# A mixer's decay matrix: from products on TensorE to rows loaded on all partitions and a bias per head

## The chip, the cores and the metric

The kernel runs on one core of a Trainium2 chip. The metric is the device time of one execution in microseconds (us). A core has five engines that run their own instruction streams in order: PE (TensorE, with its weight loads shown apart as PEld), DVE (VectorE), ACT (ScalarE), POOL (GpSimd) and SP (SyncE, which here issues nearly all DMAs). PE writes its results to PSUM, eight banks of 2 KB per partition; the other data lie in SBUF, 128 partitions wide, or in DRAM.

## The reference

The model has two layers on x of 16 sequences x 128 tokens x 256 channels, with a context of the same shape. Layer 0 is an mLSTM mixer with the context as keys and values, then a mixture of experts (two shared experts and the best two of eight). Layer 1 is a cross attention of 16 heads, then a mixture of sixteen experts. The change concerns the first mixer. For each of 16 batches and 8 heads of 32 channels it computes, with q the normed x and k = v = the context:

```
cs        = cumsum(log_sigmoid(fg))                  # per head, along the 128 tokens
log_D     = cs[s] - cs[t] + ig[t], only t <= s       # else -inf
D         = exp(log_D - max_t log_D)                 # the decay matrix, 128 x 128
C         = (q k' / sqrt(32)) * D
h         = C / (max(|sum C|, exp(-max log_D)) + 1e-6) @ v
x         = x + tanh(g) * layernorm(h) * ln_scale
```

With a[t] = ig[t] - cs[t] the row maximum is cs[s] + m[s], where m is the running maximum of a. So D[t, s] = exp(a[t] - m[s]) for t <= s, and the factor 1/sqrt(32) goes into the exponent as -0.5 log 32.

## The kernel before

The 16 batches lie in four groups g of four. The first stage is one loop over steps b from -4 to 22. Step b works on batch b's scores (`mlstm_scores`, `mlstm_products`), batch b-1's values (`mlstm_values`, `mlstm_back`) and batch b-2's end (`mlstm_close`). Between these, at three places of each step (`run(b, 0)`, `run(b, 1)`, `run(b, 2)`), stand units that `at(step, place, ...)` has entered: the layer norms of a group (`ln_stats`, `apply1`, `ln_turn`), its gates (`gate_proj`, `gate_act`, `gate_scan`, `gate_spread`), the keys and values of layer 1 (`k_proj`, `v_proj`), the shared experts' pieces (`shared_gate`, `shared_up`, `shared_down`) and, from step 18, the routing of layer 0 (`route0`, moved on by `pump0`). The order is written by hand: within `manual_schedule` each of PE, DVE, ACT and POOL executes its instructions in the order in which the program writes them. SP has its DMAs in program order too.

The decay matrix is made with products. `gate_scan` builds, for a group, a tile `la` with the rows a and 1 (eight rows for each batch, in strips of 32 partitions), and a tile that `gate_spread` spreads by DVE over the heads (`rb`, L409). For a batch, two products over a strip's rows give a[t] - m[s] for four heads each in one PSUM bank (`lp0`, `lp1`, L459). A product in bf16 of the identity with the mask `caus` adds -1e30 where t > s (L462). ACT takes the exponential of a bank into SBUF (`dm`, L467). Then `mlstm_products` (L481, L487) makes q k' of half the heads in banks `qp0` and `qp1`, and DVE multiplies by `dm` into `ct`.

```
nc.tensor.matmul(t, la[rows, :], rb[rows, ...], start=True, stop=False)   # L459
nc.tensor.matmul(t, identb, caus, start=False, stop=True)                 # L462
nc.scalar.activation(t, lp[j], AF.Exp)                                    # L467
nc.vector.tensor_tensor(half[0], qp[j], half[1], ALU.mult)                # L487
```

PSUM has two banks tagged `tp` (transposes, gates, values), two tagged `e` (k, v and shared pieces), `lp0`, `lp1`, `qp0`, `qp1`. An fp32 product is two MATMUL instructions in the trace.

After the loop come the 39 expert tiles of layer 0 (`tile_in`, `tile_up`, `tile_down`; L851 in `lp` and `qp` banks, L869 in `e`), the last shared pieces, and layer 1. The expert weights' DMAs (L815) are issued at step 17, where the mixer's tiles are given up. Loads of the first stage are all issued at the start: x, the context by group (`load_c`) and by batch (`load_v`, then two steps ahead), the shared experts' weights (3 MB) and small ones.

Of the kernel before, what the change touches and what calls it, by code (L numbers as in the profile page):

```python
# [12 lines left out]
F32 = mybir.dt.float32  # L13
# [54 lines left out]
def flamingo_kernel(ctx: ExitStack, tc: tile.TileContext, a: dict, out: bass.AP):  # L68
# [9 lines left out]
    identb = cst.tile([P, P], BF16, name="identb")  # L78
    make_identity(nc, identb)
# [3 lines left out]
    caus = cst.tile([P, 4, P], BF16, name="caus")  # L83
# [3 lines left out]
        pattern=[[0, 4], [1, P]], channel_multiplier=-1,  # L87
# [67 lines left out]
    def new_xnT(g):  # L155
        return res.tile([P, KC, TG], F32, tag="xnT", name="xnT", bufs=3)
# [80 lines left out]
    load_c(2)  # L237
# [6 lines left out]
    for e in range(NSH):  # L244
# [8 lines left out]
    for g in range(2, G):  # L253
        load_x(g)
# [6 lines left out]

    xn_d = dr.tile([B * S, D], F32, name="xn_d")
# [19 lines left out]

    e32 = s1c.tile([P, 32], F32, name="e32")
    nc.vector.tensor_reduce(e32, ident.rearrange("p (i c) -> p c i", c=32), AX.X, ALU.add)
    rowm = s1c.tile([P, 3], F32, name="rowm")
    nc.vector.tensor_reduce(rowm[:, 0:1], e32[:, 0:NH0], AX.X, ALU.add)
    nc.vector.tensor_reduce(rowm[:, 1:2], e32[:, NH0 : 2 * NH0], AX.X, ALU.add)
    first, second, add_a = (rowm[:, i : i + 1] for i in range(3))  # L290

    nc.vector.scalar_tensor_tensor(add_a, second, -0.5 * math.log(DH0), first, ALU.mult, ALU.add)

    hsel = s1c.tile([P, 2, NH0 // 2], F32, name="hsel")
    nc.vector.tensor_tensor(
        hsel, e32[:, NH0 : 2 * NH0].rearrange("p (k j) -> p j k", j=2),
        e32[:, 0:NH0].rearrange("p (k j) -> p j k", j=2), ALU.subtract,
    )
# [92 lines left out]
    def gate_scan(g):  # L391
# [7 lines left out]
        la = s1.tile([P, S], F32, name="la")  # L399
        nc.vector.tensor_scalar(la, av, second, add_a, ALU.mult, ALU.add)  # L400
        nc.vector.tensor_tensor(cs, cs, mx, ALU.add)
        nc.vector.tensor_scalar(mx, mx, first, second, ALU.mult, ALU.add)
        gate_g[g] = (la, mx, cs)

    def gate_spread(g):
        la, mx, m = gate_g[g]
        rb = s1.tile([P, NH0, S], F32, name="rb")
        hs = hsel.rearrange("p j k -> p (j k)")
        nc.vector.tensor_tensor(  # L409
            rb, mx.unsqueeze(1).to_broadcast([P, NH0, S]), bc(hs, [P, NH0, S]), ALU.mult  # L410
        )
        mt = s2p.tile([P, P], F32, tag="tp", name="mt", bufs=2)
        nc.tensor.transpose(mt, m, ident)
        en = s1.tile([P, GB, 32], F32, name="en")
        nc.scalar.activation(en.rearrange("p i r -> p (i r)"), mt, AF.Exp, scale=-1.0)
        gate_g[g] = (la, rb, en)

    def k_proj(g, o):
        ps = s2p.tile([P, TG], F32, tag="e", name="kps", bufs=2)
# [12 lines left out]
    def v_proj(g, pr):  # L432
        ps = s2p.tile([P, 2, D], F32, tag="e", name="vps", bufs=2)
# [18 lines left out]
    def mlstm_scores(b):  # L452
        g, i = divmod(b, GB)
        la, rb, _ = gate_g[g]
        rows = ts(i, 32)
        lp = []
        for j in range(2):
            t = s2p.tile([P, NH0 // 2, S], F32, tag=f"lp{j}", name="lp")
            nc.tensor.matmul(  # L459
                t, la[rows, :], rb[rows, j * NH0 // 2 : (j + 1) * NH0 // 2, :], start=True, stop=False  # L460
            )
            nc.tensor.matmul(t, identb, caus, start=False, stop=True)  # L462
            lp.append(t)
        dm = []
        for j in range(2):
            t = s1.tile([P, NH0 // 2, S], F32, tag="dm", name="dm", bufs=2)
            nc.scalar.activation(t, lp[j], AF.Exp)  # L467
            dm.append(t)
        ct = [s1.tile([P, NH0 // 2, S], F32, tag="ct", name="ct", bufs=4) for j in range(2)]
        hT_b[b] = (dm, ct)  # L470
        mlstm_products(b, 0)

    def mlstm_products(b, ph):

        g, i = divmod(b, GB)
        dm, ct = hT_b[b]
        qp = [s2p.tile([P, NH0 // 2, S], F32, tag=f"qp{j}", name="qp")[:, 0:KC, :] for j in range(2)]
        for c in range(KC):
            for j in range(2):
                rows = ts(2 * ph + j, DH0)  # L480
                nc.tensor.matmul(  # L481
                    qp[j][:, c, :], cx_g[g][rows, c, ts(i, S)], xnT_g[1, g][rows, c, ts(i, S)],
                    start=True, stop=True,
                )
        for j in range(2):
            half = [t.rearrange("p (c h) s -> p h c s", h=2)[:, ph] for t in (ct[j], dm[j])]
            nc.vector.tensor_tensor(half[0], qp[j], half[1], ALU.mult)  # L487
        if ph == 1:
            hT_b[b] = ct

    def mlstm_values(b):
# [3 lines left out]
        for k in range(NH0 // 2):  # L495
            for j in range(2):
                nc.tensor.matmul(  # L497
                    hp[ts(j, 2 * DH0), k, :], vv[:, 2 * k + j, :], ct[j][:, k, :],
# [6 lines left out]
    def mlstm_back(b):  # L505
# [5 lines left out]
        en = gate_g[g][2][:, i, 0:NH0]  # L511
# [27 lines left out]
    def shared_gate(g, f):  # L539
        e, f_ = divmod(f, HC0)  # L540
        gp = s2p.tile([P, TG], F32, tag="e", name="gp", bufs=2)
# [8 lines left out]
    def shared_up(g, f):  # L550
        e, f_ = divmod(f, HC0)
        up = s2p.tile([P, TG], F32, tag="e", name="up", bufs=2)
# [8 lines left out]
    def shared_down(g, e, t):  # L561
        yp = s2p.tile([P, D], F32, tag="e", name="yp", bufs=2)
# [30 lines left out]
    def route0():  # L593
# [11 lines left out]
        pre = s2p.tile([P, B, E0], F32, tag="lp0", name="pre")  # L605
# [990 lines left out]
```

## Time and profile before

| | us |
|---|---|
| median of three runs | 1031.11 (1023.12 to 1031.48) |
| the profiled execution's own time | 1025.47 |
| its span in the trace | 1023.8 |
| PE busy | 937.5 (92%) |
| PE weight loads | 564.5 (55%) |
| DVE busy | 481.6 (47%) |
| ACT busy | 347.0 (34%) |
| POOL busy | 216.7 (21%) |
| mean granted TensorE clock | 0.939 of full speed |

Busy time is the time in which at least one instruction of the engine ran. A group's row gives busy time in us and mean ns of one instruction, then the engine's idle time just before them and what ended it. The granted clock is the share of full speed that PE had. A window's row gives a stretch, its length, and for each engine busy time and number of instructions in it.

The first lp product starts at 28.1 us and the last batch's at 262.5 us; the first expert tile's products start at 347 us, the first gather of layer 0's results is at 588.5 us.

### The profile page before, as it was taken

To read this page: it belongs to the slowest core of one execution; us is meant where nothing else is said; L and a number is where in the kernel's file an instruction comes from. 1 tells how busy PE (TensorE), PEld (TensorE's weight loads), DVE (VectorE), ACT (ScalarE), POOL (GpSimd) and SP (SyncE) were. 2 spreads that over 40 slices of the span, in tenths; PEclk is the share of its full clock that TensorE was granted. 3 is DMA by queue.
4 is the path that set the end of the run, shared out by engine and by line. 5 is a ranking of instruction groups with operands and counts; after the bars stand their busy time and mean duration, and the time that the engine had idled before them with its cause. 6 is when DMAs were issued, how large, how long until landed. Compare 5 with 4: busy or idle time off the path is not lost.

```text
span 1023.8 us, 13944 instructions
## 1 busy us (share of the span) xinstructions
PE 937.5 (92%) x4510; PEld 564.5 (55%) x4524; DVE 481.6 (47%) x1756; ACT 347.0 (34%) x807; POOL 216.7 (21%) x318
## 2 busy tenths in 40 slices
PE   4999999999998999999999987979889898988996
PEld 2555555655554556656655554545555555555553
DVE  2555454434336422222222145786858665733534
ACT  2342424233210221121122115665454433544540
POOL 3122011001000211111110043432110233053505
PEclk9896999898999999999999995989989799999998
DMA  8692100000049211111111048113000002243523
GB/s 274 233 309 87 61 6 31 6 6 21 1 160 353 86 52 44 47 46 42 47 47 32 26 132 299 43 31 105 21 21 1 23 33 81 77 135 117 175 71 118
DMA packets 63510, 89.59 MB, mean 88 GB/s; under 512 B 9328, under 2 KB 48880, under 8 KB 62928
## 3 DMA queue, kind: packets, MB, share of 16 engines
q1 hardware_dynamic: 56960, 70.74, 20.9%
q0 software_dynamic: 6480, 17.97, 5.7%
q8 instruction: 38, 0.62, 0.3%
q14 instruction: 32, 0.26, 0.1%
HBM read 56.26 MB, written 32.42 MB: 87 GB/s over the span
## 4 chain that ended last, share of the span: by engine, by line
PE 78%; DVE 10%; issue 4%; ACT 4%; DMA 2%; POOL 1%; SPq 1%; POOLq 0%; DVEq 0%; ACTq 0%
PE typ L869 7%; PE tgp L851 7%; PE tup L851 7%; PE gp L543 6%; PE gu L1317 6%; PE yp L564 5%; PE up L554 5%; PE lp L459 3%; PE tp L1039 3%; PE yp L1346 3%; PE sp L1013 3%; PE qp L481 2%; PE yps L1107 2%; PE hp L497 2%; PE ln_tp L355 2%
## 5 line engine op out<-in xcount | busy, mean ns | idle before, releaser
L1032 ACT ACTIVATE sc<-sc,mx 128x128 f32<-128x128 f32 x256 | 78.3, 388 | 41.2 <-DVE mx L1026 41.2
L822 POOL DMA_INDIRECT xt<-xn_d,ti x39 | 39.7, 1018 | 209.1 <-PE xtp L837 164.3
L851 PE MATMUL tgp<-w1e,xT 128*128 x156 | 79.5, 593 | 0.3 <-issue 0.3
L869 PE MATMUL typ<-w2e,thT 128*128 x312 | 76.8, 389 | 0.7 <-ACT thT L866 0.7
L1317 PE MATMUL gu<-wgu,xT 128*128 x152 | 72.9, 602 | 2.8 <-POOL ln_rs L336 1.7
L851 PE MATMUL tup<-w3e,xT 128*128 x156 | 73.3, 592 | 0.0
L869 PEld LDWEIGHTS typ<-w2e,thT 128*128 128x128 f32 x312 | 56.1, 189 | 30.9 <-ACT thT L866 24.9
L543 PE MATMUL gp<-xnT,w 128*128 128x512 f32 x128 | 68.2, 660 | 0.3 <-ACT sg L547 0.3
L858 DVE TENSOR_TENSOR h<-tup,tsg 128x512 f32<-128x512 f32 x39 | 27.0, 692 | 86.5 <-PE tup L851 83.9
L564 PE MATMUL yp<-w,hT 128*128 128x256 f32 x256 | 63.3, 406 | 1.7 <-DVE x L568 1.7
L856 ACT ACTIVATE tsg<-tgp 128x512 f32<-128x512 f32 x39 | 23.3, 598 | 120.6 <-PE tgp L851 120.6
L554 PE MATMUL up<-xnT,w 128*128 128x512 f32 x128 | 60.5, 595 | 0.0
L564 PEld LDWEIGHTS yp<-w,hT 128*128 128x128 f32 x256 | 51.7, 205 | 11.4 <-DVE x L568 2.1
L873 DVE COPY ys<-typ 128x256 f32<-128x256 f32 x39 | 16.6, 425 | 87.1 <-PE typ L869 87.1
L558 DVE TENSOR_TENSOR hT<-up,sg 128x512 f32<-128x512 f32 x32 | 22.1, 691 | 73.7 <-PE up L554 69.9
L1026 DVE CUSTOM_DVE_ANT_0 sc<-sp,mb 128x128 f32<-128x128 f32 x256 | 56.3, 286 | 0.8 <-PE sp L1013 0.8
L1013 PE MATMUL sp<-kz,qT 32*128 32x256 f32 x256 | 50.5, 455 | 6.2 <-DVE mx L1026 5.7
L851 PEld LDWEIGHTS tup<-w3e,xT 128*128 128x128 f32 x156 | 29.6, 190 | 36.9 <-issue 36.8
L1039 PE MATMUL tp<-ident,sc 128*128 128x128 f32 x256 | 43.9, 316 | 6.0 <-ACT pT L1042 4.2
L547 ACT ACTIVATE sg<-gp 128x512 f32<-128x512 f32 x32 | 19.1, 598 | 88.8 <-PE gp L543 82.8
L487 DVE TENSOR_TENSOR ct<-qp,dm 128x256 f32<-128x256 f32 x64 | 24.3, 420 | 50.9 <-PE qp L481 47.5
L702 POOL DMA_INDIRECT yg<-ys_d,si x32 | 33.3, 1040 | 63.4 <-DMA ys_d<-ys 42.8
(290 smaller groups left out, 1660.1 us busy)
## 6 DMA issues: line engine op xcount, KB each, us to landing
xs<-zero SPq DMA_DIRECT2D x2, 2584.0 KB
xt<-xs SPq DMA_DIRECT2D x38, 136.0 KB
ys_d<-ys SPq DMA_DIRECT2D x39, 128.0 KB
ys<-ys SPq DMA_DIRECT2D x38, 128.0 KB
kz_d<-kst SPq DMA_DIRECT2D x8, 512.0 KB
va_d<-vs SPq DMA_DIRECT2D x8, 512.0 KB
w1e<-in_L_ffn_w_T_dram SPq DMA_DIRECT2D x8, 512.0 KB
w3e<-in_L_ffn_w_T_dram SPq DMA_DIRECT2D x8, 512.0 KB
```

The source lines that it names most:

```text
L543: nc.tensor.matmul(gp, shw[e][0][:, c, ts(f_, P)], xnT_g[2, g][:, c, :], start=(c == 0), stop=(c == KC - 1))
L554: nc.tensor.matmul(up, shw[e][1][:, c, ts(f_, P)], xnT_g[2, g][:, c, :], start=(c == 0), stop=(c == KC - 1))
L564: nc.tensor.matmul(yp, sh_g[g, e * HC0 + f][:, ts(t, P)], shw[e][2][:, f, :], start=(f == 0), stop=(f == HC0 - 1))
L702: nc.gpsimd.indirect_dma_start(out=yg, out_offset=None, in_=ys_d[:, :], in_offset=bass.IndirectOffsetOnAxis(ap=si_j[j][:, b : b + 1], axis=0),
L822: nc.gpsimd.indirect_dma_start(out=xt, out_offset=None, in_=xn_d[:, :], in_offset=bass.IndirectOffsetOnAxis(ap=ti[:, i : i + 1], axis=0), ...
L851: nc.tensor.matmul(ps, xT[:, c, :], w_[:, bass.ds(ev + c * HID0, HID0)], start=(c == 0), stop=(c == KC - 1),)
L869: nc.tensor.matmul(yp, hT[:, f, :], w2e[:, bass.ds(ev + f * D, D)], start=(f == 0), stop=(f == HC0 - 1))
L1013: nc.tensor.matmul(sp[r][:, c], qT_g[g][rows, c, ts(i, S)], kz_g[g][rows, c, :, ts(i, S)], start=True, stop=True,)
L1026: nc.vector.tensor_tensor_reduce(out=sc[:, k, :], in0=sp[:, k // 2, k % 2, :], in1=masks[g][:, i, :], scale=1.0, scalar=3.0e38, op0=ALU.ad ...
L1032: nc.scalar.activation(sc[:, k, :], sc[:, k, :], AF.Exp, scale=-1.0, bias=mx[:, n : n + 1])
L1039: nc.tensor.transpose(tp[:, k, :], sc[:, k, :], ident)
L1317: nc.tensor.matmul(gu, xT[:, c, :], wgu[:, bass.ds(ev + c * NGRP * 2 * GW, 2 * GW)], start=(c == 0), stop=(c == KC - 1),)
```

## The change

The rows m[s] no longer go through PE. `gate_scan` makes -m - 0.5 log 32 and stores it to a DRAM tile `m_d`, one per group. At the end of step b, `mlstm_load(b + 2)` loads a batch's eight rows back onto all 128 partitions (512 KB in SBUF). In step b, `mlstm_decay(b + 1, q)` works in two parts: with q = 0 DVE adds the mask `caus` (now fp32, 128x128) to all eight heads' rows; with each q ACT takes the exponential of four heads, one instruction per head, with a[t] of the head as a bias column. The bias columns come from `gate_turn`, which turns the rows a and the rows for the normalizer on PE, in place of `gate_spread`. The products of a step (`mlstm_scores(b, q)`) take two of eight heads' strips as before, in another order of `ct`.

The banks `lp0` and `lp1` go to the tag `e`, which has four now. The expert tiles' L851 products take `e` banks and L869 takes `qp`. The routing's small products move to `qp0`, `qp1` and `e`. The gates of groups 1 to 3 start one step earlier (four buffers of `xnT` in place of three), the k and v units of groups 1 and 2 are placed anew (from step -1 on), and the loads of the third context piece, of x for groups 2 and 3 and of the shared weights move from the start into steps 0 to 3.

```diff
-    identb = cst.tile([P, P], BF16, name="identb")
-    make_identity(nc, identb)
...
-    caus = cst.tile([P, 4, P], BF16, name="caus")
+    caus = cst.tile([P, P], F32, name="caus")
...
-        return res.tile([P, KC, TG], F32, tag="xnT", name="xnT", bufs=3)
+        return res.tile([P, KC, TG], F32, tag="xnT", name="xnT", bufs=4)
...
-    load_c(2)
...
-    for e in range(NSH):
+    def load_shared(e):
...
-    for g in range(2, G):
-        load_x(g)
...
+    m_d = [dr.tile([P, S], F32, name=f"m_d{g}") for g in range(G)]
...
-    e32 = s1c.tile([P, 32], F32, name="e32")
...
-        la = s1.tile([P, S], F32, name="la")
-        nc.vector.tensor_scalar(la, av, second, add_a, ALU.mult, ALU.add)
         nc.vector.tensor_tensor(cs, cs, mx, ALU.add)
-        nc.vector.tensor_scalar(mx, mx, first, second, ALU.mult, ALU.add)
-        gate_g[g] = (la, mx, cs)
-
-    def gate_spread(g):
-        la, mx, m = gate_g[g]
-        rb = s1.tile([P, NH0, S], F32, name="rb")
-        hs = hsel.rearrange("p j k -> p (j k)")
-        nc.vector.tensor_tensor(
-            rb, mx.unsqueeze(1).to_broadcast([P, NH0, S]), bc(hs, [P, NH0, S]), ALU.mult
-        )
-        mt = s2p.tile([P, P], F32, tag="tp", name="mt", bufs=2)
-        nc.tensor.transpose(mt, m, ident)
+        nc.vector.tensor_scalar(mx, mx, -1.0, -0.5 * math.log(DH0), ALU.mult, ALU.add)
+        sync.dma_start(out=m_d[g], in_=mx)
+        gate_g[g] = (av, cs)
+
+    def gate_turn(g):
+        mt = s2p.tile([P, 2, P], F32, tag="tp", name="mt", bufs=2)
+        for i, t in enumerate(gate_g[g]):
+            nc.tensor.transpose(mt[:, i, :], t, ident)
+        at_ = s1.tile([P, P], F32, name="gaT")
+        nc.vector.tensor_copy(at_, mt[:, 0, :])
         en = s1.tile([P, GB, 32], F32, name="en")
-        nc.scalar.activation(en.rearrange("p i r -> p (i r)"), mt, AF.Exp, scale=-1.0)
-        gate_g[g] = (la, rb, en)
+        nc.scalar.activation(en.rearrange("p i r -> p (i r)"), mt[:, 1, :], AF.Exp, scale=-1.0)
+        gate_g[g] = (at_, en)
...
-    def mlstm_scores(b):
...
-            nc.tensor.matmul(
-                t, la[rows, :], rb[rows, j * NH0 // 2 : (j + 1) * NH0 // 2, :], start=True, stop=False
-            )
-            nc.tensor.matmul(t, identb, caus, start=False, stop=True)
...
-            nc.scalar.activation(t, lp[j], AF.Exp)
...
+    def mlstm_load(b):
         g, i = divmod(b, GB)
+        t = s1.tile([P, NH0, S], F32, tag="dm", name="dm", bufs=3)
+        sync.dma_start(out=t, in_=m_d[g][i * 32 : i * 32 + NH0, :].partition_broadcast(P))
+        dm_b[b] = t
+
+    def mlstm_decay(b, q):
+        g, i = divmod(b, GB)
+        t = dm_b[b]
+        if q == 0:
+            nc.vector.tensor_tensor(t, t, caus.unsqueeze(1).to_broadcast([P, NH0, S]), ALU.add)
+
+        for h in (2 * q, 2 * q + 1, 2 * q + 4, 2 * q + 5):
+            n = i * 32 + h
+            nc.scalar.activation(t[:, h, :], t[:, h, :], AF.Exp, bias=gate_g[g][0][:, n : n + 1])
+
+    def mlstm_scores(b, q):
...
         for j in range(2):
-            half = [t.rearrange("p (c h) s -> p h c s", h=2)[:, ph] for t in (ct[j], dm[j])]
-            nc.vector.tensor_tensor(half[0], qp[j], half[1], ALU.mult)
+            nc.vector.tensor_tensor(ct[:, 2 * q + j], qp[j], dm[:, 2 * q + j], ALU.mult)
...
-        gp = s2p.tile([P, TG], F32, tag="e", name="gp", bufs=2)
+        gp = s2p.tile([P, TG], F32, tag="e", name="gp", bufs=4)
...
-        tp = s2p.tile([P, 2, NT0], F32, tag="qp0", name="tok")
+        tp = s2p.tile([P, 2, NT0], F32, tag="e", name="tok", bufs=4)
...
-        at(s0 - 4, 1, (ln_stats, k1, s1))
+        s0 = GB * g - (g > 0)
+        at(s0 - 4, 0, (ln_stats, k1, s1))
...
-        at(s0 - 1, 0, (gate_spread, g))
+        at(s0 - 2, 2, (gate_turn, g))
+        s0 = GB * g
...
-        at(1 + e, 1, (shared_scale, e))
+        at(1 + 2 * e, 0, (load_shared, e))
+        at(4 + e, 0, (shared_scale, e))
+    for g in range(2, G):
+        at(2 * g - 3, 2, (load_x, g))
+    at(0, 2, (load_c, 2))
...
-    for i, u in enumerate(kv[1] + kv[2]):
-        at(i // 2, (0, 1)[i % 2], u)
+    rest = kv[1] + kv[2]
+    for p in (-2, -1, 0, 1, 3, 4, 6, 9):
+        at(*divmod(p, 3), rest.pop(0))
...
-                mlstm_scores(b)
+                mlstm_scores(b, 0)
             run(b, 0)
             if 0 <= b < NB:
-                mlstm_products(b, 1)
+                mlstm_scores(b, 1)
             if 0 <= b - 1 < NB:
                 mlstm_values(b - 1)
+            if 0 <= b + 1 < NB:
+                mlstm_decay(b + 1, 0)
             if 0 <= b - 2 < NB:
                 mlstm_close(b - 2)
             run(b, 1)
             if 0 <= b - 1 < NB:
                 mlstm_back(b - 1)
+            if 0 <= b + 1 < NB:
+                mlstm_decay(b + 1, 1)
             run(b, 2)
+            if 0 <= b + 2 < NB:
+                mlstm_load(b + 2)
...
-        gp = s2p.tile([P, HID0], F32, tag=f"lp{i % 2}", name="tgp")
-        up = s2p.tile([P, HID0], F32, tag=f"qp{i % 2}", name="tup")
+        gp = s2p.tile([P, HID0], F32, tag="e", name="tgp", bufs=4)
+        up = s2p.tile([P, HID0], F32, tag="e", name="tup", bufs=4)
...
-        yp = s2p.tile([P, D], F32, tag="e", name="typ", bufs=2)
+        yp = s2p.tile([P, D], F32, tag=f"qp{i % 2}", name="typ")
```

## Prediction

> **What bounds the kernel now.** I first read the list of costliest groups, then the windows by stage, then the instructions in order of time. The change touches the first stage, 28 us (first lp product) to 278 us (end of the last), and the 68 us behind it up to the first expert tile. In the windows (columns: stretch, its length, busy time and instructions of PE, PE's weight loads, DVE, ACT, POOL, granted clock, DMA share, GB/s) these are the steps 0 to 6, the steps 7 to 15, and the rest:
>
> ```profile
> 28.10:120.80 92.70, 88.43 (x528) 50.76 (x532) 47.78 (x140) 33.29 (x52) 18.21 (x29) 0.83 0.52 180
> 120.80:278.50 157.70, 151.80 (x745) 89.67 (x754) 68.45 (x196) 51.58 (x72) 14.30 (x33) 0.92 0.04 12
> 278.50:346.00 67.50, 59.18 (x226) 34.45 (x225) 35.28 (x94) 9.64 (x16) 6.41 (x8) 0.95 0.59 200
> ```
>
> PE is busy 95% and 96% of the first two; DVE 52% and 43%, ACT 36% and 33%. PE's own work sets the pace, at a granted clock under 1. Next, what one batch's decay products cost in order of time (step 7, full clock):
>
> ```profile
> 120.76 1.12 PE L459 MATMUL lp<-rb,la 32*128 32x512 f32 x2
> 122.13 1.12 PE L459 MATMUL lp<-rb,la 32*128 32x512 f32 x2 [0.25 <-issue]
> 123.18 0.10 PEld L462 LDWEIGHTS <-identb 128*128 128x128 bf16 x1 [0.76 <-issue]
> 123.19 0.39 PE L462 MATMUL lp<-caus,identb 128*128 128x512 bf16 x1
> 123.50 0.71 PE L481 MATMUL qp<-xnT,ctxT 32*128 32x128 f32 x8
> ```
>
> From the first lp product to the next work (qp) PE spends 123.50 - 120.76 = 2.74 us. (Only 18 of the 32 caus products are recorded; their places are still in the gaps.) The groups give the rest of what I use: lp, its exponentials, rb, and the same exponential form as the new one:
>
> ```profile
> L459 PE MATMUL lp<-rb,la 32*128 32x512 f32 x64 | 37.8, 671 | 3.3 <-issue 3.3
> L467 ACT ACTIVATE dm<-lp 128x512 f32<-128x512 f32 x32 | 18.5, 596 | 37.3 <-PE lp L462 11.7 <-PE pb L510 11.0 <-remote 4.9
> ...
> L409 DVE TENSOR_TENSOR rb<-gmx,hsel 128x1024 f32<-128x1024 f32 x4 | 4.9, 1216 | 0.0
> ...
> L1032 ACT ACTIVATE sc<-sc,mx 128x128 f32<-128x128 f32 x256 | 78.3, 388 | 41.2 <-DVE mx L1026 41.2
> ```
>
> **Removed from PE.** Four products and their gaps per batch: 15 x 2.74, and 5.08 us in step 5, where the chain shows the block at half clock (81.40 to 86.48): 46.2 us, all on the engine that sets the pace. Added: gate_turn transposes two rows instead of one, 4 x 0.30 us (the mt row, L413) = 1.2. **PE: -45 us.**
>
> **DVE.** Added: per batch caus plus the loaded rows, 128x1024 f32. The nearest row is rb, same form, 1.216 us: 16 x 1.216 = 19.5; four copies out of PSUM at 0.35 (the gmn row, L388) = 1.4. Removed: rb 4 x 1.216, la 4 x 0.32 = 6.1. **+15 us**; 5.1 us of time would remain if nothing else held DVE up, since DVE has half its time free, but it counts in the early steps (below).
>
> **ACT.** Eight exponentials of 128x128 with a bias column replace two of 128x512. L1032 is the same form: 388 ns alone, 78.3 / 256 = 306 ns back to back. Per batch 2.45 to 3.1 us against 1.19: +20 to +31 us over 16; I take 22, as they come in fours. They stand in two places of a step, with the shared pieces' Silu between them. Writing out the order of Exp, Ln and Silu by step, I count 9 loads for Silu before, as many as the trace has up to 310 us; after it 14, and 5 more for Exp: +10 loads. In the trace a load is 1.283 us and the next activation starts 0.14 behind it (196.94 to 198.36): +14 us. In steps 7 to 15 ACT goes from 52 of 158 us to 52 + 9 x 1.3 + 14 = 78 of about 134. It still has slack, and two shared pieces can now stand in four banks while ACT is late. So I cost ACT at 2 us there. Without that cover each late Silu would hold PE about 1.4 us.
>
> The Trainium skill, "ScalarE: Activation LUTs", section "What ACT_TABLE_LOAD costs", puts a switch at 1283 ns for the load and about 1380 ns of drain. The trace agrees on the first and shows 0.14 us where the second would be. By the skill the ten would be an estimated 26.6 us of ACT instead of 14, and ACT 90 of 134 us.
>
> **DMA and SP.** Added: 16 loads of 512 KB, every partition reading one batch's 4 KB, and four 64 KB stores: 8.7 MB, 24 us at the 360 GB/s that the trace reaches, over 230 us, and 20 issues of 0.43 us on SP. No load of this size from one 4 KB piece is in the trace. From above: the 128 KB broadcast of lsg landed 4.82 us after its issue, beside other traffic at 359 GB/s; four times that is 19 us. From below: x0, 512 KB, was used 4.26 us after its issue. I take 4.3, as that is the row with the same size. Below zero it can't go. A load is issued at the end of a step and used in the middle of the next, so 4 to 8 us are free. The shared weights (3 MB), half of x and the third context piece move from the start into steps 0 to 3: at step 1 some 3.6 MB come in (10 us at 360 GB/s), which fits within two steps. SP passes m_d's store only when DVE's scan is done; behind it wait the first v piece's store and batch 0's load.
>
> **Batch 0.** The scan ends at 26.3; store, then readable 2.6 us later (a ys store issued at 585.88 is gathered at 588.5); load 4.3; add 1.2; four exponentials 1.3: dm at 35.7, against 31.9 for the first ct now, 3.8 us late. Behind the add wait apply1 of group 1 and so PE's ln_turn; behind the exponentials the k evictions. PE has k and v pieces of group 1 moved ahead of it (four pieces, 7 us), in four banks. I count 0 lost, with 4 as upper end.
>
> **Early steps, 0 to 6.** What is late next is DVE. Its work by step after the change, from the rows of each piece: 5, 7.4, 6.5, 9.7, 6.7, 12.5, 8 = 56 us, in order, with PE waits between (ct, back). PE: 88.4 - 20.8 (lp) - 3.6 (two k pieces now ahead of step 0) = 64, of which about 13 is lost clock. So the step can't fall by all of 2.74: adding step by step whichever of DVE or PE is longer, with 1 to 1.5 us of waits each, step 7 starts near 110 instead of 123.5 (-13.5); PE alone would give -20. I take -15.
>
> **Later steps, 7 to 15.** 9 x 2.74 = 24.7 off PE, less one transpose and 2 for ACT: -22. PE stays the bound (127 of 135 us).
>
> **Rest.** The 67.5 us behind are the routing chain on DVE, the expert weights' DMA and the last shared pieces. They start earlier and keep their length; the four banks may fill part of PE's 8.3 idle us: 0 to -3, I take -1. The expert tiles swap their banks two for two: 0. Set-up (identb, e32, rowm: 2 us of POOL and DVE before the first data) is hidden: 0.
>
> **Sum:** -15 - 22 - 1 = -38 on the profiled execution, 1025.5 us (span 1023.8): 987.5. The three timed runs lie at 1023 to 1031, mean 1028.6, so I forecast their kind at 990.
>
> **Rivals.**
> *The clock takes it.* At 75 to 93 us PE runs at half clock for 17 us, with at most 0.7 us of 3 idle:
>
> ```profile
> 78.00:81.00 3.00, 2.31 (x20) 1.91 (x16) 2.79 (x10) 0.59 (x1) 0.62 (x1) 0.50 0.43 132
> 81.00:84.00 3.00, 3.00 (x6) 0.74 (x4) 2.60 (x11) 0.00 (x0) 2.08 (x4) 0.50 0.00 0
> 84.00:87.00 3.00, 3.00 (x8) 1.06 (x9) 0.32 (x1) 0.74 (x2) 1.01 (x3) 0.50 0.13 44
> ```
>
> With products gone and waits in, more steps may run so. If all early steps had the 0.68 of steps 4 and 5, PE's 51 us of full-clock work would take 75, and steps 7 to 15 at the 0.76 of step 10 would take 162 instead of 158: about -13 + 4 = -9, 1016 to 1020. For it: lighter work. Against it: several lp blocks stand right ahead of a half-clock stretch (171 to 182, 225 to 235), so the products that go may be light work themselves; then up to half of the 27 us lost to the clock from 28 to 278 comes back, 975. Chance 0.13 the bad way; 0.08 the good way.
> The Trainium skill, "TensorE: Matmul & The Clock Gate", section "Why this matters for your kernels", asks for no PE idle gaps over about 3 us between bursts, as the clock drops behind one. Here it drops with gaps under 1 us, so the trace doesn't bear out the bound, only the direction.
>
> *ACT becomes the bound of steps 7 to 15*, by loads and exponentials in order ahead of Silu: if each of the 10 added loads holds PE 1.4 us, 14 us are given back: 1003. Chance 0.14; ACT's 58% share speaks against it.
>
> *The readback is late in each step: slower.* If one load takes 19 us (lsg's rate), the 16 loads need 304 us, where 250 are there now: +54, about 1083. It decides from 15.6 us a load (250 / 16): above that the loads, one behind the other, set the step; at 4.3 they are hidden. Against it: lsg landed in full traffic. Chance 0.06.
>
> *No gain, since another wait stood behind the products:* PE's idle time in steps 7 to 15 is 5.9 us of 158, mostly beside lp itself, so nothing else sets the pace; +-5 us of 1029, chance 0.03.
>
> **The numbers.** The forecast's own case, 980 to 1001, has 0.56. One per cent, 10 us, is about what a measurement of this kernel can tell from no change. Faster by over 1%: forecast, good clock, ACT, and half of the bad clock: 0.56 + 0.08 + 0.14 + 0.07 = 0.85; same: 0.06 + 0.03 = 0.09; slower 0.06. The range 973 to 1018 leaves out the readback, most of the no-gain case and the edges of the clock.
>
> **What would show it.** No lp row; 128 exponentials near 306 ns; the add near 1.22 us; about 16 loads for Exp and 14 for Silu; steps 7 to 15 near 135 us with PE over 90% busy; steps 0 to 6 with DVE over 75% busy. Wrong, if the wait ending last ahead of ct or the add is the DMA, if ACT is what PE's gp waits for, or if the clock from 28 us on is under 0.8.

## Result, and the profile after

The changed kernel takes 988.54 us (median of four runs, 986.27 to 989.45) against 1029.13 us (median of four, 1023.12 to 1031.48): a ratio of 0.961, 95% interval 0.956 to 0.966. The profiled execution took 986.27 us with a span of 984.5 us, 39.3 us less than the span before. The forecast was 990, between 973 and 1018. In all groups of runs below, executions more than 1.5% above the fastest of their kernel count in the medians, but not in the ratios.

Both spans are cut at the same events: the first qp product of step 0, of step 7 and of step 15, the first products of the second expert tile, the first gather of layer 0's results. The windows of the kernel before, and below them those of the kernel after (columns as in the prediction: stretch, length, PE, PE's weight loads, DVE, ACT, POOL, granted clock, DMA share, GB/s):

```profile
30.87:123.50 92.63, 88.36 (x526) 50.72 (x531) 47.78 (x140) 33.54 (x52) 18.27 (x29) 0.83 0.49 170
123.50:265.15 141.65, 137.00 (x676) 81.20 (x683) 62.06 (x179) 46.93 (x64) 13.46 (x30) 0.92 0.04 13
265.15:357.75 92.60, 82.94 (x338) 50.43 (x338) 44.69 (x120) 15.31 (x24) 9.22 (x12) 0.96 0.48 164
588.50:1023.80 435.30, 384.32 (x2021) 234.43 (x2019) 261.48 (x1170) 195.27 (x575) 132.76 (x172) 0.93 0.27 87
```

```profile
32.27:111.45 79.18, 62.74 (x486) 43.87 (x485) 51.25 (x138) 46.97 (x105) 16.67 (x26) 0.87 0.86 282
111.45:226.54 115.09, 110.02 (x635) 69.06 (x634) 68.10 (x185) 68.32 (x120) 13.27 (x31) 0.97 0.14 45
226.54:319.31 92.77, 83.32 (x339) 50.71 (x339) 45.38 (x122) 14.17 (x21) 11.52 (x15) 0.96 0.50 170
550.10:984.50 434.40, 383.88 (x2017) 233.92 (x2015) 259.95 (x1169) 194.22 (x575) 132.69 (x172) 0.92 0.27 87
```

Steps 7 to 15 (second line) shrink by 26.6 us, and PE is still busy 96% of them. Steps 0 to 6 (first line) shrink by 13.5 us but start 1.4 us later, so step 7 starts 12.05 us earlier; here PE is now idle for 16 of 79 us, where it was idle for 4 of 93. The stretch from step 15 on is as long as before to within 0.2 us, and so is everything behind it to within 1 us.

The new operations in the list of costliest groups of the kernel after, first 310 us (instruction, shapes, count, then busy us and mean ns, then idle time ahead and what ended it):

```profile
L448 ACT ACTIVATE dm<-dm,gaT 128x128 f32<-128x128 f32 x128 | 40.4, 390 | 15.5 <-DVE dm L444 15.4
L444 DVE TENSOR_TENSOR dm<-dm,caus 128x1024 f32<-128x1024 f32 x16 | 19.4, 1214 | 5.6 <-DMA dm<-m_d 5.6
L523 ACT ACT_TABLE_LOAD x15 | 19.2, 1283 | 11.9 <-PE gp L519 11.7
L448 ACT ACT_TABLE_LOAD x14 | 18.0, 1283 | 0.2
```

The 128 exponentials take 40.4 / 128 = 316 ns each, back to back. Of the 16 adds one alone ever waits for its rows, for 5.6 us: batch 0's. This is that place in order of time, in the kernel after (start, duration, engine, line, operation; SPq is SP's queue; idle time ahead in brackets):

```profile
27.08 0.34 SPq L383 DMA_DIRECT2D m_d<-gmx  x1
27.71 3.23 SPq L423 DMA_DIRECT2D va_d<-vs  x2
31.03 1.70 SPq L437 DMA_DIRECT2D dm<-m_d  x3
...
36.18 1.23 DVE L444 TENSOR_TENSOR dm<-dm,caus 128x1024 f32<-128x1024 f32 x1 [5.63 <-DMA dm<-m_d]
37.33 0.73 DVE L324 TENSOR_SCALAR xn<-x,ln_mv,ln_rs 128x256 f32<-128x256 f32 x2
38.46 0.75 DVE L465 TENSOR_TENSOR ct<-qp,dm 128x256 f32<-128x256 f32 x2 [0.41 <-ACT dm L448]
...
37.88 1.09 PE L336 MATMUL ln_tp<-ident,xn 128*128 128x128 f32 x4 [4.90 <-DVE xn L324]
```

From the store of the rows to the add that uses them 9.1 us go by. DVE stands idle in front of the add, the normalizations of group 1 (L324) stand behind it on DVE, and PE stands idle until they are done. Later the loads land 3.3 to 8.4 us after their issue, median 5.3 (of the 13 whose landing is recorded), and nobody waits for them.

PE's stand costs more than its length. The windows of it and of the 6 us behind it, in the kernel after:

```profile
33.00:36.00 3.00, 0.00 (x0) 0.00 (x0) 0.00 (x0) 0.00 (x0) 0.00 (x0) 1.00 0.97 254
36.00:39.00 3.00, 1.12 (x5) 1.15 (x6) 2.41 (x5) 1.56 (x5) 0.00 (x0) 0.60 1.01 230
39.00:42.00 3.00, 3.00 (x8) 2.12 (x7) 0.86 (x3) 3.00 (x8) 0.00 (x0) 0.50 1.08 389
```

Behind the 4.9 us of standing the granted clock is 0.50 for some 7 us (0.76 from 42 to 45 us). The same comes twice more in these steps, behind stands of 3.65 us (up to 72.79; 0.50 from 72 to 75 us) and 2.41 us (up to 90.27; 0.50 from 93 to 96 us); in the rest of the time from 27 to 123 us the clock is 1.00.

### The profile page after: what moved, and what is told of

It reads as the page before. It is cut to its first block, busy times and chain, and to the rows that moved or that the text cites. A ratio compares the mean times of both kernels' runs of the same rounds, so it can differ in the third digit from the quotient of the medians.

```text
span 984.5 us, 13890 instructions
## 1 busy us (share of the span) xinstructions
PE 888.0 (90%) x4432; PEld 547.3 (56%) x4432; DVE 490.3 (50%) x1763; ACT 379.0 (38%) x913; POOL 215.5 (22%) x316
## 5 line engine op out<-in xcount | busy, mean ns | idle before, releaser
L1306 PE MATMUL gu<-wgu,xT 128*128 x152 | 75.4, 620 | 3.7 <-POOL ln_rs L317 2.6
L840 PE MATMUL tup<-w3e,xT 128*128 x156 | 73.3, 592 | 0.0
L540 PE MATMUL yp<-w,hT 128*128 128x256 f32 x256 | 58.1, 381 | 0.7 <-DVE hT L534 0.7
L540 PEld LDWEIGHTS yp<-w,hT 128*128 128x128 f32 x256 | 47.8, 190 | 9.0 <-issue 1.6
L855 ACT COPY thT<-htp 128x512 f32<-128x512 f32 x39 | 22.8, 586 | 69.4 <-PE htp L853 69.4
L448 ACT ACTIVATE dm<-dm,gaT 128x128 f32<-128x128 f32 x128 | 40.4, 390 | 15.5 <-DVE dm L444 15.4
## 6 DMA issues: line engine op xcount, KB each, us to landing
xs<-zero SPq DMA_DIRECT2D x2, 2584.0 KB, 13.5
```

The lines of the kernel that those rows point to most:

```text
L448: nc.scalar.activation(t[:, h, :], t[:, h, :], AF.Exp, bias=gate_g[g][0][:, n : n + 1])
L540: nc.tensor.matmul(yp, sh_g[g, e * HC0 + f][:, ts(t, P)], shw[e][2][:, f, :], start=(f == 0), stop=(f == HC0 - 1))
L840: nc.tensor.matmul(ps, xT[:, c, :], w_[:, bass.ds(ev + c * HID0, HID0)], start=(c == 0), stop=(c == KC - 1),)
L1306: nc.tensor.matmul(gu, xT[:, c, :], wgu[:, bass.ds(ev + c * NGRP * 2 * GW, 2 * GW)], start=(c == 0), stop=(c == KC - 1),)
```

## Experiments

All segments below come from one profile of each kernel, cut at the first qp product of steps 1, 7 and 15; the time is the median of its timed runs, the ratio is against the kernel before on the same chip. e1 to e4 ran on one chip, e5 to e8 on a second, e9 to e12 on a third. The kernel before ran at 1029.1, 1024.2, 1022.6 and 1021.7 us (medians) in the four groups of runs.

| kernel | us | ratio (95%) | start to step 1 | 1 to 7 | 7 to 15 (clock) | 15 to end |
|---|---|---|---|---|---|---|
| before | 1029.1 | 1 | 40.4 | 83.1 | 141.7 (0.92) | 758.7 |
| after | 988.5 | 0.961 (0.956-0.966) | 49.2 | 62.2 | 115.1 (0.97) | 758.0 |
| e1_two_banks | 996.7 | 0.972 (0.965-0.980) | 49.3 | 66.3 | 115.9 (1.00) | 767.0 |
| e2_order_alone | 1015.5 | 0.994 (0.989-0.998) | 45.2 | 69.2 | 134.8 (0.96) | 759.7 |
| e3_rows_from_start | 985.3 | 0.966 (0.961-0.971) | 39.5 | 62.0 | 114.4 (0.99) | 763.7 |
| e4_exps_together | 999.5 | 0.978 (0.972-0.984) | 48.2 | 66.2 | 118.2 (0.99) | 764.9 |
| e5_after_again | 989.2 | 0.969 (0.964-0.974) | 47.6 | 62.4 | 112.7 (1.00) | 760.0 |
| e6_mask_on_pool | 989.0 | 0.969 (0.965-0.974) | 46.8 | 67.3 | 110.5 (1.00) | 761.5 |
| e7_apply_first | 986.8 | 0.966 (0.961-0.971) | 45.4 | 62.1 | 114.4 (0.99) | 760.8 |
| e8_products_back32 | 1036.9 | 1.015 (1.009-1.020) | 51.0 | 78.6 | 143.2 (0.94) | 758.5 |
| e9_pool_queue | 990.7 | 0.970 (0.966-0.974) | 49.7 | 64.2 | 115.2 (0.97) | 761.1 |
| e10_before_again | 1021.4 | 1.000 (0.997-1.003) | 40.4 | 83.3 | 140.3 (0.93) | 756.0 |
| e11_order_again | 1012.6 | 0.993 (0.989-0.997) | 45.3 | 74.9 | 134.8 (0.96) | 756.0 |
| e12_apply_first_again | 986.0 | 0.967 (0.962-0.971) | 45.9 | 64.4 | 112.7 (1.00) | 758.6 |

The last column is nearly the same code in all of them (the banks of the expert tiles differ) and spreads over 11 us; of it layer 1, the same code everywhere, takes 434 to 445 us at a granted clock of 0.93 to 0.90. Differences of the whole below some 8 us between two kernels are therefore read from the segments, not from the times. The profile of e1 is of an execution of 1000.31 us, of a kernel that took 985 to 1000.

### The order alone: e2, e11, and the kernel before once more: e10

e2 keeps the products, their exponentials and their banks, and takes over the new order, the four buffers of xnT and the moved loads (its mask tile, in bf16 as before, lies in the mixer's part of SBUF). Against the kernel before:

```diff
-        return res.tile([P, KC, TG], F32, tag="xnT", name="xnT", bufs=3)
+        return res.tile([P, KC, TG], F32, tag="xnT", name="xnT", bufs=4)
...
-        at(s0 - 4, 1, (ln_stats, k1, s1))
+        s0 = GB * g - (g > 0)
+        at(s0 - 4, 0, (ln_stats, k1, s1))
...
-        at(s0 - 1, 0, (gate_spread, g))
+        at(s0 - 2, 2, (gate_spread, g))
+        s0 = GB * g
...
+        at(1 + 2 * e, 0, (load_shared, e))
...
+    for p in (-2, -1, 0, 1, 3, 4, 6, 9):
+        at(*divmod(p, 3), rest.pop(0))
```

> The kernel before, with its products and banks, but with the new order: gates of groups 1 to 3 a step earlier, k and v units of groups 1 and 2 placed anew, loads of shared weights, x and the third context piece in steps 0 to 3, four buffers of xnT. Theory (the gain is the products' PE time, 45 us, and the order only fills the start): 1025 to 1031 us. Rival (order and moved loads bring a good part of the 40 us): 1005 to 1018 us.

It measured 1015.53 us, ratio 0.9935 (0.989 to 0.998). That is in the rival's range of times, but the kernel before ran at 1024.2 us beside it, not at 1029: as a gain, 7 to 9 us, it lies between the two. The order, which the prediction had priced at nothing, is worth some 8 us by itself. e11 is the same kernel again and e10 the kernel before, both without an edit, to see whether that is the kernel or the execution.

> The kernel before, for a second profile. Theory A (the order's gain is a higher granted clock in steps 0 to 6, 0.83 before and 0.96 with the new order alone): steps 0 to 6 again near 92 us at a clock under 0.88. Theory B (the one profile of before had a low clock there by chance): steps 0 to 6 at 80 to 87 us, clock over 0.9.

> The kernel before with the new order alone, for a second profile. Theory A: steps 0 to 6 again near 80 us at a clock over 0.93. Theory B: longer than 85 us, at a clock under 0.9.

Windows of steps 0 to 6, and of 7 to 15, in e2:

```profile
34.68:114.39 79.71, 74.29 (x517) 45.28 (x524) 44.73 (x131) 31.28 (x49) 18.68 (x26) 0.96 0.57 191
114.39:249.18 134.79, 130.75 (x674) 76.50 (x681) 60.86 (x178) 48.33 (x66) 14.60 (x30) 0.96 0.04 13
```

the same in e11:

```profile
34.74:120.18 85.44, 79.91 (x517) 48.79 (x525) 44.45 (x131) 31.30 (x49) 18.93 (x26) 0.88 0.54 178
120.18:255.01 134.83, 130.79 (x674) 76.53 (x682) 60.85 (x178) 48.35 (x66) 14.62 (x30) 0.96 0.04 13
```

and steps 0 to 6 in e10:

```profile
30.86:123.66 92.80, 88.54 (x527) 50.59 (x532) 47.72 (x140) 33.54 (x52) 18.28 (x29) 0.83 0.48 169
```

The kernel before gives 92.8 us at 0.83 a second time, as theory A had it. e11 came out as theory B had it: the new order with the same products gives 79.7 us at 0.96 in one execution and 85.4 us at 0.88 in another, on another chip. So neither holds alone: the length of the early steps follows the granted clock, which is higher with the new order both times, but not by a fixed amount. In steps 7 to 15 the same order and the same products take 134.8 us at 0.96 twice, against 141.7 at 0.92 and 140.3 at 0.93. Time multiplied by the mean clock is the same for both orders: 1024.2 x 0.935 = 958 and 1021.7 x 0.936 = 956 for before in the two groups, 1015.5 x 0.947 = 962 and 1012.6 x 0.947 = 959 for e2 and e11; single runs of the kernel before lie from 951 to 962. So no saving of work by the order can be seen; it gets some 0.011 more clock. Why it does, these runs don't show.

### The products put back: e1 and e8

e1 is the kernel after with two banks for the shared, k and v pieces, as before:

```diff
-        gp = s2p.tile([P, TG], F32, tag="e", name="gp", bufs=4)
+        gp = s2p.tile([P, TG], F32, tag="e", name="gp", bufs=2)
...
-        yp = s2p.tile([P, D], F32, tag=f"qp{i % 2}", name="typ")
+        yp = s2p.tile([P, D], F32, tag="e", name="typ", bufs=2)
```

(the same in `k_proj`, `v_proj`, `shared_up` and `shared_down`; the expert tiles use `lp` and `qp` as before).

> The changed kernel, but the shared pieces (and the k and v pieces) have two banks again instead of four; the two banks left over lie idle in the first stage. Theory (four banks cover ACT, whose Silu comes late behind ten more table loads and the exponentials): PE waits for ACT in steps 7 to 15, up to 1.4 us for each added load, 14 us: about 1000 us, all of the loss between the steps 7 and 15, with PE's first shared product waiting for the Silu's activation. Rival (two banks were enough, as before the change, where PE waited 1.1 us for them in all): 988 us plus or minus 3.

The time, 996.67 us, is nearer to the theory's 1000 than to the rival's 988, but only a small part of it has the reason given. Steps 7 to 15, where PE was to wait 14 us for Silu, take 115.9 us at a granted clock of 1.00; e5 and e12, with four banks and the same clock, take 112.7. The list of waits of e1, PE alone, 110 to 235 us (total us, number, longest), has

```profile
PE yp L540 <- ACT sg L523: 2.1, 2, 1.1
PE mt L389 <- DVE gav L377: 2.0, 1, 2.0
PE gps L355 <- ACT xnT L337: 1.5, 1, 1.5
PE gp L519 <- ACT sg L523: 1.3, 2, 1.1
```

3.4 us of waits for ACT's `sg`; after has none of them. The other differences of e1's profile are 4 us in steps 1 to 7 and 9 us behind step 15, and neither is seen to come from the banks. In step 4 a load of rows is late: SP's issue of a `kz_d` store at 58.21 us takes 4.18 us, batch 4's load is issued at 63.76 us (59.81 in the kernel after), the add waits 3.73 us for it, and PE stands 7.48 us in place of 3.65. The 9 us are layer 1's, which the edit does not touch: 445.1 us at a clock of 0.90, against 434.4 at 0.92; the expert tiles take 230.4 us, against 230.8. The intervals of e1 and e5 overlap (0.965-0.980, 0.964-0.974). So the two added banks are seen to be worth some 3 us, in one profile, and not 14.

e8 adds to e1 the four products per batch in their old sizes and places, on data at hand; nobody reads their result.

```diff
+        for j in range(2 if q == 0 else 0):
+            t = s2p.tile([P, 4, S], F32, tag=f"lp{j}", name="lp")
+            nc.tensor.matmul(
+                t, cx_g[g][ts(i, 32), j, ts(i, S)], xnT_g[1, g][ts(i, 32), j, :], start=True, stop=False
+            )
+            nc.tensor.matmul(t, identb, causb, start=False, stop=True)
```

> The kernel with two banks for the shared pieces, and in each batch products of the old shape back on PE (32 rows, 128x512, fp32 and a bf16 one) in the two idle banks, read by nobody; nothing else is changed and the outputs are those of the reference. It prices PE time in the new order. Theory (PE sets the pace in steps 7 to 15, DVE and the rows in the early ones): the span from step 7 to 15 grows by 8 x 2.74 = 22 us against the two-bank kernel's 116, the early steps by under 10 of the 19 us. Rival (PE's time sets both): both by all, 41 us, as slow as the kernel before. Second rival (light products lower the clock, which costs more than their time): over 45 us.

It measured 1036.93 us, ratio 1.015 (1.009 to 1.020), slower than the kernel before, and 40 us above e1 (33 between the two profiles, as e1's end was long). Step 7 starts 13.9 us later than in e1. Steps 7 to 15 of e1, then of e8, which hold eight blocks:

```profile
115.68:231.54 115.86, 107.88 (x636) 68.15 (x635) 68.22 (x185) 68.21 (x120) 13.36 (x31) 1.00 0.13 44
```

```profile
129.57:272.80 143.23, 137.68 (x684) 78.90 (x683) 68.50 (x185) 68.43 (x120) 13.46 (x30) 0.94 0.11 35
```

PE's busy time times the clock goes from 107.9 to 137.68 x 0.94 = 129.4: 21.5 us for eight blocks, 2.69 each, against the 2.74 that the prediction read. But the stretch grows by 27.4 us, as the clock goes from 1.00 to 0.94 with the products. Here the products cost their own time and, on top, a quarter of it in clock. The 22 us that I had expected of these steps were low, and so were the under 10 for the early ones (13.9 at the start of step 7); the rival's total of 41 was right.

### The readback: e3, e7, e9, e12

e3 loads the rows from a constant DRAM piece that is there from the start; the same bytes move, no load waits for a scan. The kernel leaves out the real rows, so its decay matrix is not the mixer's and the routing of layer 0 sees other numbers.

```diff
+    m_c = dr.tile([NH0, S], F32, name="m_c")
+    sync.dma_start(out=m_c, in_=neg)
...
-        sync.dma_start(out=t, in_=m_d[g][i * 32 : i * 32 + NH0, :].partition_broadcast(P))
+        sync.dma_start(out=t, in_=m_c.partition_broadcast(P))
```

> The changed kernel, but every batch's rows are loaded from a DRAM piece of constants that is written at the start, so no load waits for the scan's rows and their store; the same 16 loads of 512 KB, the same sums and exponentials. The decay matrix is left wrong, and the routing of layer 0 sees other numbers. Theory (the readback is late once, for batch 0, where PE stands 4.9 us until 37.9 us; later loads are covered): 4 to 6 us faster than the changed kernel, about 983.5 us, all of it before step 1. Rival (loads are late in every early step, as DMA is near full there): 8 us or more, spread over steps 0 to 6; or, if PE's stand at 33 to 38 us is DVE's and not the load's: nothing, 988 us.

Its windows from the first qp of step 0 (to within 0.1 us) to that of step 1, and on to that of step 7:

```profile
30.11:39.53 9.42, 8.26 (x105) 6.52 (x104) 4.96 (x10) 8.02 (x21) 0.14 (x1) 1.00 0.83 308
39.53:101.54 62.01, 52.40 (x382) 35.83 (x381) 44.73 (x126) 38.45 (x83) 15.42 (x24) 0.86 0.93 306
```

Step 0 of the kernel after:

```profile
32.27:49.23 16.96, 10.90 (x105) 8.37 (x105) 6.54 (x12) 8.51 (x22) 0.00 (x0) 0.80 0.98 307
```

Step 1 starts at 39.5 us in place of 49.2, and from there step 7 is 62.0 us away, as in after (62.2). Of these 9.7 us, 7.5 lie in step 0 (9.4 us in place of 17.0; e5, the kernel after once more, takes 16.6): 4.9 are idle time of PE, and 2.6 are the same 105 products at a clock of 0.80 in place of 1.00. The other 2.2 lie ahead of step 0, where nothing waits for rows; e1 and e4, which read the rows back, start step 0 at 30.8 and 30.0 us, as early as e3. So the readback costs some 7.5 us, all of it at batch 0, more than the 4 to 6 expected, and in the kernel after the other 15 loads cost nothing (in e1 one more was late). The whole shows less of it: 985.3 us, and a ratio between after's two (0.961 and 0.969); e3's profile gives back 5.7 us behind step 15.

e7 moves the normalizations of group 1 ahead of the add that waits:

```diff
-        at(s0 - 4, 2, (apply1, g, 0))
-        at(s0 - 3, 0, (ln_turn, k1, 0, s2p), (apply1, g, 1))
+        if g != 1:
+            at(s0 - 4, 2, (apply1, g, 0))
+        at(s0 - 3, 0, (ln_turn, k1, 0, s2p))
+        if g != 1:
+            at(s0 - 3, 0, (apply1, g, 1))
...
+    at(-1, 0, (apply1, 1, 0), (apply1, 1, 1))
```

> The changed kernel, but group 1's two normalizations stand on DVE ahead of the sum that waits for batch 0's rows. Theory (PE stands 33 to 38 us only because the transposes need what is queued behind that sum): PE does the first transposes and a v piece meanwhile, step 1 starts 2 to 3 us earlier and so does all behind it. Rival (the rows' arrival itself bounds step 0: the first decay product, then q k' of the other heads, whose banks wait for it): step 1 as before, 49 us, 0 gained.

Against e5, the kernel after run beside it, step 1 starts 2.2 us and step 7 2.5 us earlier: as expected. e12 is e7 once more, beside e9:

> The kernel with group 1's normalizations first, for a comparison with the one with POOL's queue on the same chip. Expected as measured before: 0.966 of the kernel before; by the theory on the queue 3 us slower than that with POOL's queue, by its rival the same.

It shows the four normalizations in the place where DVE stood idle:

```profile
30.14 1.51 DVE L324 TENSOR_SCALAR xn<-x,ln_mv,ln_rs 128x256 f32<-128x256 f32 x4 [0.91 <-POOL ln_rs L318]
34.80 1.23 DVE L444 TENSOR_TENSOR dm<-dm,caus 128x1024 f32<-128x1024 f32 x1 [3.15 <-DMA dm<-m_d]
```

Its lead over e5 is 1.7 us at step 1 and 2.5 at step 6 (87.97 against 90.47), as e7's is; but its step 7 starts at 110.35, 0.4 us later than e5's. The second half of its step 6, the same 69 products and no wait of PE among them, is this in e7 and in e12 (windows):

```profile
94.81:107.49 12.68, 12.68 (x69) 8.03 (x68) 6.65 (x16) 8.19 (x14) 2.29 (x5) 1.00 0.52 174
```

```profile
95.98:110.35 14.37, 14.37 (x69) 8.88 (x68) 6.67 (x16) 8.19 (x14) 2.30 (x5) 0.88 0.47 147
```

12.68 / 0.88 = 14.4: the lead went to the clock of that execution (e12 ran on another chip than e5 and e7). The two times, 986.77 and 986.02 us, are the lowest of all kernels that compute the decay matrix; 2 to 3 us below e5 are what was expected, but lie inside the intervals.

e9 adds to e7 that batch 0's store and load go through POOL's queue, past the two stores of `va_d` on SP's:

```diff
-        sync.dma_start(out=m_d[g], in_=mx)
+        (nc.gpsimd if g == 0 else sync).dma_start(out=m_d[g], in_=mx)
...
-        sync.dma_start(out=t, in_=m_d[g][i * 32 : i * 32 + NH0, :].partition_broadcast(P))
+        (nc.gpsimd if b == 0 else sync).dma_start(out=t, in_=m_d[g][i * 32 : i * 32 + NH0, :].partition_broadcast(P))
```

> The kernel with group 1's normalizations first (the run before last of the last four), and batch 0's chain of store and load issued on POOL's DMA queue instead of SP's, so that neither stands behind the v pieces' stores nor behind the bulk loads in SP's queue. Theory (of the 9 us from the scan's end to the rows' arrival, half is queueing behind other traffic): rows 3 to 5 us earlier, near 32 us, step 1 near 42 us instead of 45.4, 3 us faster in all. Rival (the time is that of two dependent DMAs through DRAM, with whatever queue): rows at 35 us or later, nothing gained.

My theory fell. In order of time, e9:

```profile
26.65 0.80 POOL L383 DMA_DIRECT2D m_d<-gmx  x1 [17.86 <-DVE gmx L382]
30.49 0.58 POOL L437 DMA_DIRECT2D dm<-m_d  x1 [3.04 <-DMA m_d<-gmx]
...
39.28 1.22 DVE L444 TENSOR_TENSOR dm<-dm,caus 128x1024 f32<-128x1024 f32 x1 [5.25 <-DMA dm<-m_d]
```

The wait for the store's landing stays: from the store to the load's issue 3.84 us go by without the `va_d` stores in between, 3.96 with them (e12), and POOL stands 3.04 us for it. The rows are there 8.8 us after the load's issue, where SP's queue took 5.1 (e12: issue at 29.71, add at 34.80). Step 1 starts 3.8 us later than in e12; the rival's "nothing gained" is right.

### DVE and ACT: e5, e6 and e4

e5 is the kernel after without an edit, as the neighbour for e6, e7 and e8.

> The changed kernel as it is, for a comparison on the chip of the next three. Every theory: 0.961 of the kernel before, and step 7 starting near 111 us.

989.21 us against 988.54; its ratio, 0.969 (0.964 to 0.974), is above the first one because the kernel before was faster in these runs (1022.6 us). The gain is thus 33 to 41 us by the group of runs.

e6 gives the mask's add to POOL, which takes it off DVE:

```diff
-            nc.vector.tensor_tensor(t, t, caus.unsqueeze(1).to_broadcast([P, NH0, S]), ALU.add)
+            nc.gpsimd.tensor_tensor(t, t, caus.unsqueeze(1).to_broadcast([P, NH0, S]), ALU.add)
```

> The changed kernel, but the mask is added on POOL instead of DVE: 16 x 1.21 us off DVE, 16 sums of 128x1024 on POOL (the shared weights' scaling, 128x1024, took 2.9 us there). Theory (DVE's work in order is what PE waits for in steps 2 to 6, and in step 0 everything queued behind the sum that waits for the rows): step 7 starts 4 to 8 us earlier, near 105 us; the later steps, where DVE is 59% busy, as before. Rival (the exponentials come 1.7 us later in each step and PE waits for them): step 7 at 111 us or later, and 0 to 10 us slower in all.

The row of the add, and two waits between 24 and 115 us, in e6:

```profile
L444 POOL TENSOR_TENSOR dm<-dm,caus 128x1024 f32<-128x1024 f32 x16 | 37.8, 2362 | 4.4 <-DMA dm<-m_d 4.4
...
DVE ct L465 <- ACT dm L448: 7.1, 1, 7.1
PE qp L460 <- DVE ct L465: 4.7, 2, 4.4
```

The add takes 2.36 us in place of 1.21, and in step 0 DVE now waits 7.1 us for `dm` and PE 4.4 for `ct`. Steps 1 to 7 take 67.3 us in place of 62.4, though DVE has only 41.4 us of work in them instead of 44.7: as the rival had it. What less work on DVE would be worth by itself e6 doesn't show, as it also makes each `dm` later. In steps 7 to 15, with DVE 6 us lighter, 2.3 us are gained, and the whole stays where it was.

e4 lets both halves of the exponentials follow each other:

```diff
                 mlstm_decay(b + 1, 0)
+                mlstm_decay(b + 1, 1)
...
-            if 0 <= b + 1 < NB:
-                mlstm_decay(b + 1, 1)
```

> The changed kernel, but the eight exponentials of a batch stand in one place of the step (behind the mask's sum) instead of two, so fewer table loads lie between Exp and Silu: by the written order about 20 loads instead of 29 in the first stage, 11 to 13 us less ACT time. Theory (ACT has slack and the four banks cover it): 986 to 990 us, no change that can be measured. Rival (ACT sets part of the later steps): 975 to 981 us.

The two groups of loads in e4, to hold against the 15 and 14 of after:

```profile
L523 ACT ACT_TABLE_LOAD x11 | 14.1, 1283 | 9.9 <-PE gp L519 9.7
L448 ACT ACT_TABLE_LOAD x9 | 11.5, 1283 | 0.2
```

Nine loads fewer in these groups, and ACT is busy 61.2 us in place of 68.3 in steps 7 to 15; yet these steps take 118.2 us, 3 to 5 us more than in after and e5, and the kernel is not faster (999.52 us), which neither expectation had. The table loads were not what set the pace. Against e7, at the same clock of 0.99 (114.4 us), these steps lose 3.7 us, and 3 of them are longer waits of PE for DVE (2.1 us for `hT`, 0.9 in e7; 1.9 ahead of `gps`, where e7 has none). Why the whole is 10 us slower is not settled.

## Why the prediction was right

The total was right to 1.5 us, and the mechanism, work taken off the engine that sets the pace, is what the runs show. That the total came so near was partly luck: two terms that the forecast put at nothing, the wait at batch 0 and the granted clock, cancelled.

**PE's 45 us.** Right, if at the upper end. PE's busy time fell from 937.5 to 888.0 us. e8 gives 2.69 us of full-clock work a block against 2.74; by the windows of steps 7 to 15 above, 137.0 x 0.92 against 110.0 x 0.97, it is 19.3 us for eight blocks, 2.4 each.

**Early steps, -15.** Measured -12.05 at the start of step 7, as a sum of other terms. The prediction took PE's own 20 us and cut them to 13.5 to 15, since DVE would be late next; it counted nothing for batch 0 and nothing for the clock. By the windows of steps 0 to 6, PE's work at full clock falls by some 19 us (88.4 x 0.83 = 73.3 to 62.7 x 0.87 = 54.5), as forecast. PE's idle time in steps 1 to 6 grows by 6.1 us (4.3 to 10.4), which is about what was taken off for DVE; 7.1 of the 10.4 are waits for DVE. The list of PE's waits, 32 to 112 us of the kernel after, begins with

```profile
PE ln_tp L336 <- DVE xn L324: 9.6, 3, 4.9
PE mt L389 <- DVE gav L377: 2.4, 1, 2.4
```

of which the 4.9 us are batch 0's. (DVE's share of the time was lower than forecast, 65% of steps 0 to 6 against over 75%.) What came on top is the clock: PE lost 15.0 us to it in these steps before and 8.2 after. With the readback out of the way (e3) step 7 starts at 101.5 us, 22 us earlier than before.

Against that stands **the mis-sized step, "Batch 0": "I count 0 lost, with 4 as upper end"**: 7.5 us by e3, and with it the prediction's own sign of being wrong, an add that waits last for the DMA, came true at this one place. The rows were later than taken: scan end 27.05 in place of 26.3; from store to load's issue 3.95 us in place of 2.6; from issue to add 5.15 in place of 4.3; so the first `ct` is at 38.46, not at 35.7, 2.8 us late. The rest is the cover: I had PE fed by k and v pieces meanwhile, but PE is idle up to 37.88, as `ln_turn` hangs on the normalizations behind the add, and then works at half clock; step 0 takes 17.0 us where e3 needs 9.4.

Of the -12, the order by itself gives 3.3 to 9.1 (e11, e2), mostly through the clock. The prediction had no term for it.

**Later steps, -22.** Measured -26.6 from step 7's first qp to step 15's, a stretch with eight blocks (21.9 us at full clock). The mechanism was right; the clock, 0.92 to 0.97, was left out. By e2 (134.8) the order gives 6.9 of it and the removal the other 19.7; by e8 against e1 the products are worth 27.4. The two differ mostly by the clock that each profile happened to have (0.96 and 0.97; 0.94 and 1.00). PE stayed the bound, 96% busy.

**ACT at 2 us.** In the kernel after no wait of PE between 110 and 235 us is on ACT's `sg`. The largest three:

```profile
PE mt L389 <- DVE gav L377: 2.0, 1, 2.0
PE gps L355 <- ACT xnT L337: 1.5, 1, 1.5
PE pb L486 <- ACT hs L478: 0.7, 1, 0.7
```

ACT's busy time up to the second expert tile went from 105.5 to 138.6 us: +33 against +36 forecast. The exponentials are +21.9, as taken; the loads, 15 for Silu (14 forecast) and 14 for Exp (about 16), are nine more than the 10 and 10 before, and the activation behind a load starts 0.01 to 0.02 us after it in 25 of 27 cases from 111 to 320 us, not 0.14 as I had taken from one place. The Trainium skill, "ScalarE: Activation LUTs", section "What ACT_TABLE_LOAD costs", has about 1380 ns of drain there, which this trace doesn't show either. The rival "ACT becomes the bound" falls with these waits, and e4, with nine loads fewer, bears that out.

**DMA and SP.** The load was taken at 4.3 us and has a median of 5.3 (3.3 to 8.4), covered 15 times of 16; the readback rival would have needed 15.6. Two statements were wrong without effect on the sum, that SP has its DMAs in program order and that the shared weights come in in steps 0 to 3. In the kernel after the first shared expert's weights, written in step 1, are issued at 16.84 and 23.36 us, before step 0, and the second's, written in step 3, from 40.45 to 48.26 us, in step 0:

```profile
16.84 0.89 SPq L245 DMA_DIRECT2D w<-in_L_ffn_sw_T_dram  x2
...
23.36 0.43 SPq L249 DMA_DIRECT2D w<-in_L_ffn_sw_T_dram  x1
```

**DVE, +15.** +10.1 us of busy time up to the second expert tile (164.3 to 174.4). Its amount is not seen to count by itself; the waits for it named above are.

**Rest, -1.** +0.2, and layer 1 -0.9.

**The clock rival.** Its bad side fell: in none of the windows shown but layer 1's (0.92 against 0.93) is it lower than before. Its good side came in part, 0.83 to 0.87 and 0.92 to 0.97; that is where the late steps' extra 4 to 5 us come from, and some 7 in the early ones.

## What to carry to other kernels

Work taken off the engine that sets the pace is worth its own time, read block by block at full clock, and the granted clock moves with it: here by a tenth less to a quarter more. A round trip through DRAM is hidden only where something has been put in front of it: price the first one, which has no step before it, by following each engine's queue behind the waiting instruction until one of them runs dry, and add what the clock loses behind the stand. A sum can be right by two errors; a run that takes out a single wait (e3) shows it.

## What was not expected of the hardware

The granted clock differs between executions of one program: e2 and e11 are the same kernel, with 0.96 and 0.88 in the same steps, e7 and e12 are, with 1.00 and 0.88 over the same 69 products (each pair on two chips), and on one chip the kernel before ran from 1011.5 us at a mean clock of 0.947 to 1034.3 us at 0.924. Heavier products came with a lower clock in steps 7 to 15: 0.92 to 0.96 in the five profiles with them, 0.97 to 1.00 in the nine without. In the early steps of the kernel after, half clock came behind stands of PE of 2.4 to 4.9 us; the kernel before had it for 17 us, from 75 us on, with no stand of PE over 0.7 us.

One load through POOL's queue (e9) was slower than the same one through SP's (e12), 8.8 us against 5.1 from issue to use of its 512 KB. The same add took POOL 2.36 us and DVE 1.21.
